# Attention's result turned by VectorE, queries and new keys loaded batch by batch, and layer 2 and 3's last products reordered

## The chip, the cores and the metric

The kernel runs on one core of one Trainium2 chip. The time is device microseconds of one execution; each kernel is run several times and the median is compared. TensorE (PE in the profile) multiplies, VectorE (DVE) and ScalarE (ACT) work on elements, GpSimd (POOL) works on elements and gathers rows, and SyncE (SP) mostly issues DMAs. Each engine runs its own list of instructions in order and waits on semaphores for the others.

## The reference

Four layers, each `x = x + ffn(cond(x))`, over 8 batches of 128 tokens of 512 features, all in float32. Layers 0 and 1 are gated and low-rank products. Layer 2 holds the attention, which takes most of the time, and layers 2 and 3 end with routed low-rank products. Cut to what the change touches:

```
# layer 2, conditioning: attention over a paged cache (32 query heads, 8 key heads of 128)
q, k, v = x @ Wq.T, x @ Wk.T, x @ Wv.T        # per head
q, k = rope(rmsnorm(q)), rope(rmsnorm(k))
k_all = concat(k_cache[block_table], k); v_all = concat(v_cache[block_table], v)
probs = softmax(mask(q @ k_all.T * SCALE))    # 512 cached and 128 new keys
y2 = (probs @ v_all) @ Wo.T
# layer 2, ffn, on y2
H = y2 @ W.T + b; z = y2 @ A
logits from H[:, 1::2, :8] and (z @ LiMEs.T)[:, 1::2]; weights = masked softmax, repeated over token pairs
x = x + H + (z * (weights @ LiMEs)) @ Bmat * 0.5
# layer 3, ffn: 64 experts of rank 8, 16 of them taken
out = (gated z) @ B_w.T * 2
x = x + out
```

## The kernel before

**Attention.** It runs in 32 steps: `steps` (qd, p) with eight key heads qd on the outside and four pairs of batches p on the inside, so step 4 qd + p. A step's TensorE work is, in this order: ten score products `st` of batch 0 of the pair (`weigh`, 128x512 each, four for cached keys and one for new keys, each in two records), the projection of the next step's queries, keys and values (`project`, tiles q_one, q_six, q_five), the last step's output product (`leave`, tiles wo_one, wo_two, wo_six), the scores of batch 1 mixed with the value products of batch 0, and the value products `av` of batch 1 (`mix`). Both products with weights use a seven-product scheme for 2x2 blocks (`seven`), whose sums of blocks are made by VectorE (`combine`). A float32 matmul shows as two records in the profile.

**Queries and new keys.** `rotate` puts a step's rotated queries (2 batches x 4 heads) and new keys (2 batches x 1) side by side in the tile r, all queries first. `turn` (L1206) transposes r with one VectorE stream transpose, which works on blocks of 32x32, and writes the result to the DRAM tensor turned_new in four DMAs; `fetch` (L1234) loads it back with the blocks in their places: one DMA of 512 KB for all queries (tile qT) and one of 64 KB for each batch's new key (tile kTn). qT and kTn have one buffer each, so a load of the next step's queries waits until the last scores of this step have read the old ones. Steps 0 and 1 are turned by TensorE instead (`turn_at_once`). The cached keys go the same way through turned_cached.

**The result.** y2 (8 batches of 128 tokens by 512, in SBUF) collects the output products. In the last four steps (qd = 7) each pair p - 1 is complete once step p has run `leave`; `run` then calls `end.turn` twice (L1497), which turns one batch with four TensorE transposes into PSUM and copies it to Y2T with VectorE or ScalarE. After the last step come the h products of quarter 0 (256 tokens) with W (`product`, 16 matmuls into the tiles h_0 and h_1), the last `leave`, the turning of the last pair (`layer2`), the products hdT for the anchors (`anchors`) and z (`low`), the routing on VectorE, and the h products of quarters 1 to 3.

**Order.** `kept` fixes an instruction's place in its engine's program order; instructions without it may be moved by the scheduler that builds the program. Before, the transposes y2T, hdT, z and h were not kept, and the scheduler put four of the h products of quarter 1 between the last transposes and the first hdT. DMAs that SyncE issues run in the order of its queue; after the last step it issues R (the softmax sums, `inverted`), then the loads of Bm, W, Wq, keys, wB3T, wmr, BwT (`open3`) and the sums for a check (L833).

**Layer 3's last products.** `Seven` (L2095) does four output blocks with seven products in two PSUM banks, odd and even. For tokens of group g = 1 two of them run one after the other, k = 0 and 1 (`last`, L2244): `go_on` multiplies, with VectorE forming u and p1 between the products, then x gets its sums, and the four blocks are added to x and each sent out by a DMA on SyncE's queue (L2258, L2259).

Of the kernel before, what the change touches and what calls it, by code (L numbers as in the profile page):

```python
# [17 lines left out]
P = 128  # L18
NB = 8
# [28 lines left out]
def forward(ctx: ExitStack, tc: tile.TileContext, a: dict, out: bass.AP):  # L48
# [31 lines left out]
    ))  # L80
    late_turned = w3T, wB3T, A2T
    down_turned, adapter_turned = (
# [794 lines left out]
def attention(tc, a, x, ident, lens, kvrow, part, ww, wop, ypool, sums, rot, eps, psa, c2, chunks, mm):  # L877
# [262 lines left out]
    def rotate(n):  # L1140

        both = wk.tile([P, 2 * REP + 2, HD], F32, tag="r", name=f"r_{n}", bufs=1)
        views = {"q": both[:, 0 : 2 * REP], "k": both[:, 2 * REP :]}

        def terms(m, t, nh):

            full = [P, 2, nh, HD]
            ws, wx = (w[:, pair(n), :] for w in tabs[m])
            r = views[m].rearrange("p (j h) d -> p j h d", j=2)
            u = wk.tile(full, F32, tag="v" + m, name=f"v{m}_{n}", bufs=1)  # L1150
            for b in ((slice(0, 1), slice(1, 2)) if nh > 1 else (slice(0, 2),)):
                for lo, hi in ((0, 64), (64, 0)):
                    to = u[:, b, :, lo : lo + 64]
                    kept(pool.tensor_tensor(  # L1154
                        to, t[:, b, :, hi : hi + 64],
                        wx[:, b, lo : lo + 64].unsqueeze(2).to_broadcast(list(to.shape)), ALU.mult,
                    ))
            def straight_terms():
                kept(dve.tensor_tensor(r, t, ws.unsqueeze(2).to_broadcast(full), ALU.mult))

            S[n]["r" + m] = r, u
            return straight_terms

        S[n]["both"] = both
        terms("q", S[n]["q"], REP)()
        return terms("k", S[n]["k"], 1)
# [39 lines left out]
    def turn(n, by=(sp,)):  # L1206

        s = S[n]
        m = 2 * REP
        t = wk.tile([P, 4, m + 2, 32], F32, tag="kt", name=f"qkt_{n}", bufs=1)  # L1210
        done = kept(dve.transpose(t, s["both"].rearrange("p m (b d) -> p b m d", b=4)))
        s["qT"] = wk.tile([P, 4, m, 32], F32, tag="qT", name=f"qT_{n}", bufs=1)
        s["kn"] = wk.tile([P, 2, 4, 32], F32, tag="kTn", name=f"kTn_{n}", bufs=1)
        written(turned_new[n], t, by)
        return done

    def turn_at_once(n):

        s = S[n]
        m = 2 * REP  # L1220
        s["qT"] = qT = wk.tile([P, 4, m, 32], F32, tag="qT", name=f"qT_{n}", bufs=1)
        s["kn"] = kn = wk.tile([P, 2, 4, 32], F32, tag="kTn", name=f"kTn_{n}", bufs=1)
        for h in (slice(0, REP), slice(REP, m), slice(m, m + 2)):
            k = h.stop - h.start
            ps = psa.tile([P, k, P], F32, name=f"turned_{n}_{h.start}", **(
                dict(tag="av") if n == 0 and k == REP else dict(tag="st", bufs=3)
            ))
            for i in range(k):
                kept(pe.transpose(ps[:, i, :], s["both"][:, h.start + i, :], ident))
            to = qT[:, :, h, :].rearrange("p a m t -> p m a t") if k == REP else kn  # L1230
            kept(act.copy(to, ps.rearrange("p m (a t) -> p m a t", t=32)))

    def fetch(n):
        s = S[n]  # L1234
        m = 2 * REP
        src = turned_new[n].rearrange("b i a m d -> (b i) a m d")
        kept(sp.dma_start(s["qT"], src[:, :, 0:m, :]))
        for j in range(2):
            kept(sp.dma_start(s["kn"][:, j], src[:, :, m + j, :]))

    def weigh(n, j, then={}):
# [5 lines left out]
        for c in range(NC):  # L1247
            ps = psa.tile([P, REP * P], F32, tag="st", name=f"st_{n}_{j}_{c}", bufs=3)
            kept(pe.matmul(  # L1249
                ps, s["kT"][:, c, 4 * j : 4 * j + 4, :] if c < 4 else s["kn"][:, j],  # L1250
                s["qT"][:, :, REP * j : REP * (j + 1), :].rearrange("p a i t -> p i a t"), start=True, stop=True,
            ))
# [149 lines left out]
    def run(pool_, end_of, bank, keep):  # L1402
# [11 lines left out]
        w_ops, wo_ops = iter(()), WO[0].factors()  # L1414

        def some(ops, k=1):
            return lambda: [next(ops, None) for _ in range(k)]

        for n, (qd, p) in enumerate(steps):
# [75 lines left out]
            if qd == NQ - 1 and p:  # L1495
                for j in range(2):
                    end.turn(y2, 2 * (p - 1) + j, bank)  # L1497
        divided(n)
        every(outputs(n))
        end.product(0, ("st", "st"), bank)  # L1500
        leave(n)
# [312 lines left out]
def ending(  # L1814
# [64 lines left out]
    def turn(y2, b, bank):  # L1879
# [3 lines left out]
        for c in range(DC):  # L1883
            pe.transpose(ps[:, c, :], y2[:, b, c * P : (c + 1) * P], ident)
        (act.copy if b % 2 else dve.tensor_copy)(Y2T[0][:, :, b * P : (b + 1) * P], ps)

    def quarter(q):
        return slice(q * NT // 4, (q + 1) * NT // 4)

    def low(bank):  # L1890

        ps = bank("mm", [P, NT // 4], "z2")
        for c in range(DC):
            for q in range(4):
                mmq(ps[slot(q), :], A2[:, c, :], Y2T[0][:, c, quarter(q)], c == 0, c == DC - 1)
        act.copy(zq, ps)

    def anchors(bank, meanwhile):

        ps = bank("mm", [P, P], "hdT")  # L1900
        for c in range(DC):
            for q in range(4):
                mmq(ps[slot(q), :], WH[:, c, :], Y2T[0][:, c, q * NT // 4 + 1 : (q + 1) * NT // 4 : 2], c == 0, c == DC - 1)
        hdT = L3.w3.tile([P, P], F32, tag="hdT", name="hdTs")
        dve.tensor_copy(hdT, ps)
        meanwhile()
        ps = bank("mm", [P, NA, 32], "hd")
        pe.transpose(ps.rearrange("p q e -> p (q e)"), hdT, ident)
        dve.tensor_tensor(hd, ps[:, :, 0:16], b16.unsqueeze(1).to_broadcast([P, NA, 16]), ALU.add)
# [7 lines left out]

    def product(q, tags, bank, at=range(2), begun=False):

        for i, tag in zip(at, tags):  # L1920
            ps = H[q, i] if begun else bank(tag, [P, 2, NT // 4], f"h_{q}_{i}")
            for o in range(2):
                for c in range(DC):
                    mmq(
                        ps[:, o, :], W["2"][:, c, (2 * i + o) * P : (2 * i + o + 1) * P], Y2T[0][:, c, quarter(q)],
                        not begun and o == 0 and c == 0, begun and c == DC - 1,
                    )
            H[q, i] = ps

# [165 lines left out]
    class Seven:  # L2095


        def __init__(self, name, bank, A, B):
            self.A, self.B = A, B
            self.even, self.odd = (bank("mm", [P, 2, 256], f"{name}_{i}") for i in range(2))  # L2100
            self.p1, self.u = (
                L3.w3.tile([P, 256], F32, tag=f"seven_{n}", name=f"{n}_{name}", bufs=2) for n in ("p", "u")
            )
            self.c = {(0, 0): (self.even[:, 0], None), (0, 1): (self.odd[:, 1], self.u),
                      (1, 0): (self.even[:, 1], self.u), (1, 1): (self.odd[:, 0], self.p1)}

# [4 lines left out]
        def begin(self):  # L2111
            self.into(self.even[:, 0], self.A[0], self.B[0], True)
            act.copy(self.p1, self.even[:, 0])

        def go_on(self):
            a11, a12, a22, s1, s2, s3, s4 = self.A
            b11, b21, b22, t1, t2, t3, t4 = self.B
            u, p1, even, odd = self.u, self.p1, self.even, self.odd
            self.into(odd[:, 1], s1, t1, True)
            self.into(odd[:, 0], s2, t2)  # L2120
            dve.tensor_tensor(u, odd[:, 0], p1, ALU.add)
            dve.tensor_tensor(p1, odd[:, 1], p1, ALU.add)
            self.into(even[:, 1], s3, t3)
            dve.tensor_tensor(p1, even[:, 1], p1, ALU.add)
            self.into(odd[:, 1], s4, b22)
            self.into(even[:, 0], a12, b21)
            self.into(even[:, 1], a22, t4)

# [110 lines left out]
    def last_begun(g, k, bank):  # L2239

        f = S["o", g, k] = Seven(f"o3_{g}_{k}", bank, S["b"][k], S["z", g])
        f.begin()

    def last(g, k):  # L2244
        f = S["o", g, k]
        f.go_on()
        for (i, j), (ps, more) in reversed(f.c.items()):
# [3 lines left out]
            if more is not None:  # L2251
                dve.tensor_tensor(t, t, more, ALU.add)
        for ij in ((1, 1), (0, 1), (0, 0), (1, 0)):
            ps = f.c[ij][0]
            o = 2 * k + ij[0]
            tok = slice(g * 512 + ij[1] * 256, g * 512 + (ij[1] + 1) * 256)
            t = x[:, o, tok]
            dve.tensor_tensor(t, ps, t, ALU.add)  # L2258
            sp.dma_start(out[o * P : (o + 1) * P, tok], t)  # L2259

    def layer2(y2, bank, do=range(NB)):

        for b in do:
            turn(y2, b, bank)
        anchors(bank, lambda: low(bank))
        where = ["mm"]
        folding = fold_scores(lambda tag, shape, name: bank(where[0], shape, name))
        if (0, 0) not in H:
            product(0, ("st", "st"), bank)
# [17 lines left out]
    def layer3(bank, between=lambda behind: None):  # L2287
# [31 lines left out]
        for k in range(2):  # L2319
            S["o", 1, k].B = S["z", 1]  # L2320
        last(1, 0)
        last(1, 1)

    return SimpleNamespace(
        prepare=prepare, load_w2=load_w2, load_aw=load_aw, turn=turn,
        product=product, shifted=shifted, open3=open3, layer2=layer2, layer3=layer3,
    )
# [65 lines left out]
```

## Time and profile before

| | us |
|---|---|
| median of three runs (1473.62 to 1477.49) | 1475.64 |
| the profiled execution | 1473.67 |
| its span, first to last instruction | 1471.8 |
| TensorE busy in it | 1459.9 |
| VectorE, GpSimd, ScalarE busy | 1066.8, 855.2, 559.0 |
| attention steps 2 to 30, start of the scores to the next | 364.43 to 1304.80 |
| 24 transposes y2T in the last three steps | 0.87, 0.88, 0.87 |
| SyncE waiting in `fetch` for turned_new's writes | 85.0 in 58 waits |
| end of the last value product (mix) | 1328.47 |
| end of the last output product of attention | 1342.29 |
| start of the last TensorE product | 1465.54 |

The page gives for each engine the busy time and its share of the span. The chain of waits goes back from the last instruction to what released it, step by step; a row is a start, a length and what ran. In the timeline a row is a start, a length, the engine and line, the operation, output and inputs with their shapes, and in brackets how long the engine stood idle before and for what. TensorE's records overlap, since matmuls are pipelined: a record of 0.59 us for 128x512 is followed by the next 0.43 us later. PEld is the loading of TensorE's stationary operand, which runs beside the products.

### The profile page before, as it was taken

To read this page: it belongs to the slowest core of one execution; us is meant where nothing else is said; L and a number is where in the kernel's file an instruction comes from. 1 tells how busy PE (TensorE), PEld (TensorE's weight loads), DVE (VectorE), ACT (ScalarE), POOL (GpSimd) and SP (SyncE) were. 2 spreads that over 40 slices of the span, in tenths; PEclk is the share of its full clock that TensorE was granted. 3 is DMA by queue.
4 is the path that set the end of the run, shared out by engine and by line. 5 is a ranking of instruction groups with operands and counts; after the bars stand their busy time and mean duration, and the time that the engine had idled before them with its cause. 6 is when DMAs were issued, how large, how long until landed. Compare 5 with 4: busy or idle time off the path is not lost.

```text
span 1471.8 us, 17654 instructions
## 1 busy us (share of the span) xinstructions
PE 1459.9 (99%) x5333; PEld 921.6 (63%) x5333; DVE 1066.8 (72%) x2128; ACT 559.0 (38%) x1416; POOL 855.2 (58%) x877
## 2 busy tenths in 40 slices
PE   9999999999999999999999999999999999999998
PEld 7888786455555555555565555556555555657886
DVE  4675535488878887877778787777878788875575
ACT  1111101044445544454554445455444444542110
POOL 2231104477767777777677777767777776731310
PEclk9999999999999999999999999999999999999999
DMA  7430312214655544464454456444445544343001
GB/s 244 131 76 26 73 35 70 90 39 123 178 157 165 156 121 129 150 184 129 136 151 120 126 157 184 129 137 150 117 129 155 173 137 134 115 122 99 1 9 52
DMA packets 178488, 177.02 MB, mean 120 GB/s; under 512 B 72336, under 2 KB 148208, under 8 KB 178256
## 3 DMA queue, kind: packets, MB, share of 16 engines
q1 hardware_dynamic: 160208, 138.79, 32.7%
q0 software_dynamic: 17056, 36.49, 8.0%
q8 instruction: 45, 0.74, 0.2%
q10 hardware_dynamic: 1120, 0.52, 0.1%
q14 instruction: 59, 0.48, 0.1%
HBM read 132.36 MB, written 43.11 MB: 119 GB/s over the span
## 4 chain that ended last, share of the span: by engine, by line
PE 91%; DMA 3%; DVE 3%; POOL 1%; issue 1%; ACT 0%; SPq 0%; ACTq 0%; DVEq 0%; POOLq 0%
PE st L1249 17%; PE av L1301 16%; PE g L414 9%; PE q_six L1055 8%; PE q_one L1055 5%; PE q_five L1055 5%; PE wo_two L1055 5%; PE dn L414 5%; PE wo_one L1055 4%; PE wo_six L1055 4%; PE eo_l L53 3%; PE h L1834 2%; PE z L1834 2%; PE o L1834 1%; PE midp_l L53 1%; DMA qT<-turned_new 1%
## 5 line engine op out<-in xcount | busy, mean ns | idle before, releaser
L998 POOL DMA_INDIRECT kn<-in_k_cache,kvrow_k x256 | 270.8, 1058 | 77.7 <-issue 67.1
L998 POOL DMA_INDIRECT vals<-in_v_cache,kvrow_v x256 | 273.1, 1067 | 73.6 <-issue 49.5
L1301 PE MATMUL av<-pT,vals 128*128 128x512 f32 x640 | 290.6, 593 | 0.2 <-DVE oT L1311 0.2
L1253 ACT ACTIVATE pT<-st,hide 128x512 f32<-128x512 f32 x256 | 175.9, 687 | 187.2 <-PE st L1249 187.1
L1249 PE MATMUL st<-qT,kT 128*128 128x512 f32 x512 | 236.2, 594 | 1.5 <-DMA qT<-turned_new 1.4
L1301 PEld LDWEIGHTS av<-pT,vals 128*128 128x128 f32 x640 | 121.6, 190 | 152.9 <-issue 146.9
L1154 POOL TENSOR_TENSOR vq<-q,txq 128x256 f32<-128x256 f32 x128 | 121.1, 977 | 131.5 <-ACT sqq L1128 89.9
L1249 PEld LDWEIGHTS st<-qT,kT 128*128 128x128 f32 x512 | 96.4, 190 | 111.2 <-issue 99.0
L1269 DVE TENSOR_TENSOR part<-pT 128x512 f32<-128x512 f32 x128 | 88.4, 691 | 77.6 <-ACT pT L1253 73.5
L1055 PE MATMUL q_one<-q,x 128*128 128x384 f32 x256 | 93.1, 486 | 0.0
L1128 ACT ACTIVATE sqq<-q 128x128 f32<-128x128 f32 x252 | 78.2, 310 | 11.8 <-DVE q L1104 5.1
L1055 PEld LDWEIGHTS q_one<-q,x 128*128 128x128 f32 x256 | 48.6, 190 | 39.7 <-issue 14.1
L1055 PE MATMUL q_six<-q_s,xs_all 128*128 128x384 f32 x192 | 69.8, 486 | 0.0
L1109 ACT COPY q<-q_one 128x256 f32<-128x256 f32 x32 | 11.9, 372 | 148.8 <-PE q_one L1055 142.7
L1055 PE MATMUL wo_one<-o,oT 128*128 128x256 f32 x256 | 65.7, 379 | 0.0
L1249 PE MATMUL st<-qT,kTn 128*128 128x512 f32 x128 | 65.4, 593 | 0.0
L1055 PE MATMUL wo_two<-o_s,os 128*128 128x256 f32 x256 | 60.6, 380 | 0.0
L1253 ACT ACTIVATE pT<-st,rs 128x512 f32<-128x512 f32 x64 | 44.0, 687 | 38.6 <-PE st L1249 38.6
L483 POOL TENSOR_TENSOR ws<-wu 128x256 f32<-128x256 f32 (+1 forms) x9 | 6.4, 711 | 87.7 <-DMA wu<-in_WuT 87.7
L1055 PEld LDWEIGHTS wo_one<-o,oT 128*128 128x128 f32 x256 | 48.7, 190 | 13.3 <-issue 0.5
L1285 ACT COPY rows<-rows 32x32 f32<-32x32 f32 x96 | 20.7, 216 | 93.1 <-DVE rows L1280 92.3
L414 PE MATMUL g<-xs,ws 128*128 128x256 f32 (+1 forms) x240 | 55.1, 379 | 0.0
(457 smaller groups left out, 2803.5 us busy)
## 6 DMA issues: line engine op xcount, KB each, us to landing
turned_new<-qkt SPq DMA_DIRECT2D x120, 160.0 KB
turned_cached<-kt SPq DMA_DIRECT2D x128, 128.0 KB
kT<-turned_cached SPq DMA_DIRECT2D x32, 512.0 KB
R<-sums SPq DMA_DIRECT2D x32, 512.0 KB
qT<-turned_new SPq DMA_DIRECT2D x30, 512.0 KB
q<-in_WqT SPq DMA_DIRECT2D x8, 1024.0 KB
o<-in_WoT SPq DMA_DIRECT2D x8, 1024.0 KB
kn<-in_k_cache,kvrow_k POOLq DMA_INDIRECT x256, 2.9
```

Of the source, the lines that this page charges most:

```text
L53: pe.matmul(o, lhsT, rhs, start=start, stop=stop)
L414: pe.matmul(o, lhsT, rhs, start=start, stop=stop, skip_group_check=True)
L998: kept(pool.indirect_dma_start(out=d[:, c, :], out_offset=None, in_=kc if what == "k" else vc, in_offset=bass.IndirectOffsetOnAxis(ap=kvro ...
L1055: kept(pe.matmul(o, l[:, c, :], r[:, c, :], start=start and c == 0, stop=c == 1, skip_group_check=True))
L1128: kept(act.activation(sq, S[n][m][:, j, i, :], AF.Square, accum_out=S[n]["ssq"][:, j, col : col + 1]))
L1154: kept(pool.tensor_tensor(to, t[:, b, :, hi : hi + 64], wx[:, b, lo : lo + 64].unsqueeze(2).to_broadcast(list(to.shape)), ALU.mult,))
L1249: kept(pe.matmul(ps, s["kT"][:, c, 4 * j : 4 * j + 4, :] if c < 4 else s["kn"][:, j], s["qT"][:, :, REP * j : REP * (j + 1), :].rearrange( ...
L1253: kept(act.activation(pT[:, c, :, :].rearrange("p i t -> p (i t)"), ps, AF.Exp, **(dict(bias=hide[:, b, c : c + 1]) if c < 4 else dict(bia ...
L1269: kept(dve.tensor_tensor(o, l, r, ALU.add))
L1285: kept(act.copy(rows[0:32, g, :], rows[32 * g : 32 * g + 32, 0, :]))
L1301: kept(pe.matmul(ps, v[:, c, :], pT[:, c, :, :].rearrange("p i t -> p (i t)"), start=c == 0, stop=c == NC - 1, skip_group_check=True,))
L1834: return pe.matmul(o, lhsT, rhs, start=start, stop=stop, skip_group_check=True)
```

## The change

Four things are changed.

1. y2 of the first three pairs is turned by VectorE (`turned_in`): one stream transpose per batch, four DMAs per batch that write it to a new DRAM tensor y2_turned in pieces of 128 bytes, and four per batch that load it into Y2T. The last pair is still turned by TensorE.
2. Transposes y2T, products hdT, z, hd and the h products of quarters 0 to 2 are kept in program order. Of the 16 h products of quarter 0, 12 run ahead of the last `leave`, three between it and the last pair's transposes, and one after them. In VectorE's order four sums of AwT stand together ahead of the copy of hdT, and the check of the sums stands ahead of zp.
3. r holds batch 0's queries and key and then batch 1's; qT and kTn are two tiles each, one per batch, and `fetch` loads queries and key of batch 0 first, then of batch 1.
4. For the last tokens the two `Seven` are interleaved: leading products of both, sums of both, then closing products and outputs of both. The second has a third PSUM bank for its product six, its last product and output are cut in halves of 128 columns, and three of the eight outputs are issued by ScalarE.

```diff
@@ attention @@
-        both = wk.tile([P, 2 * REP + 2, HD], F32, tag="r", name=f"r_{n}", bufs=1)
-        views = {"q": both[:, 0 : 2 * REP], "k": both[:, 2 * REP :]}
+        both = wk.tile([P, 2, REP + 1, HD], F32, tag="r", name=f"r_{n}", bufs=1)
+        views = {"q": both[:, :, 0:REP], "k": both[:, :, REP:]}
...
+    def new_turned(n):
+        S[n]["qT"], S[n]["kn"] = (
+            [wk.tile(shape, F32, tag=f"{what}{j}", name=f"{what}_{n}_{j}", bufs=1) for j in range(2)]
+            for what, shape in (("qT", [P, 4, REP, 32]), ("kTn", [P, 1, 4, 32]))
+        )
...
     def fetch(n):
-        s = S[n]
-        m = 2 * REP
         src = turned_new[n].rearrange("b i a m d -> (b i) a m d")
-        kept(sp.dma_start(s["qT"], src[:, :, 0:m, :]))
         for j in range(2):
-            kept(sp.dma_start(s["kn"][:, j], src[:, :, m + j, :]))
+            m = j * (REP + 1)
+            kept(sp.dma_start(S[n]["qT"][j], src[:, :, m : m + REP, :]))
+            kept(sp.dma_start(S[n]["kn"][j][:, 0], src[:, :, m + REP, :]))
...
+        def y2_turned(p):
+            bs = (2 * p, 2 * p + 1)
+            end.turned_in(y2, bs, lambda name: kvp.tile([P, 4, DC, 32], F32, tag="kn", name=name))
...
             if qd == NQ - 1 and p:
-                for j in range(2):
-                    end.turn(y2, 2 * (p - 1) + j, bank)
+                y2_turned(p - 1)
         divided(n)
         every(outputs(n))
-        end.product(0, ("st", "st"), bank)
+        end.product(0, ("st", "st"), bank, part=slice(0, 12))
         leave(n)
@@ ending @@
+    def turned_in(y2, bs, tile_of_turned):
...
+        for b in bs:
+            t = tile_of_turned(f"y2t_{b}")
+            kept(dve.transpose(t, y2[:, b, :].rearrange("p (c k i) -> p k c i", k=4, i=32)))
+            for q in range(4):
+                kept(sp.dma_start(
+                    late_turned[3][b, :, :, q], t[32 * q : 32 * q + 32].rearrange("i k c j -> i (k c) j")
+                ))
+        for b in bs:
+            for k in range(4):
+                kept(sp.dma_start(
+                    Y2T[0][slot(k), :, b * P : (b + 1) * P],
+                    late_turned[3][b, :, DC * k : DC * (k + 1)].rearrange("i c a j -> i c (a j)"),
+                ))
...
     def layer2(y2, bank, do=range(NB)):
+        begun = (0, 0) in H
+        if begun:
+            product(0, ("st", "st"), bank, part=slice(12, 15))
         for b in do:
             turn(y2, b, bank)
+        if begun:
+            product(0, ("st", "st"), bank, part=slice(15, 16))
         anchors(bank, lambda: low(bank))
...
     class Seven:
...
         def go_on(self):
+            self.lead()
+            self.close()
...
+            for h in (slice(0, P), slice(P, 2 * P)) if self.apart else (slice(0, 2 * P),):
+                self.into(six[:, h], a22, t4[:, :, h])
...
+    def last_out(g, k):
+        f = S["o", g, k]
         for ij in ((1, 1), (0, 1), (0, 0), (1, 0)):
...
+            n = P if f.apart and ij == (1, 0) else 2 * P
+            for h in range(0, 2 * P, n):
+                by = act if g and (ij == (0, 1) or h) else sp
...
-        last(1, 0)
-        last(1, 1)
+        both = [S["o", 1, k] for k in range(2)]
+        for k, f in enumerate(both):
+            f.lead()
+            summed_up(1, k)
+        for k, f in enumerate(both):
+            f.close()
+            last_out(1, k)
```

## The prediction

> **What bounds the kernel now.** First the page's head and the slices: TensorE is busy in 99% of the span at full granted clock, so only TensorE work removed, TensorE waits removed, or the tail after its last matmul can shorten the time.
>
> ```profile
> span 1471.8 us, 17654 instructions
> PE 1459.9 (99%) x5333; PEld 921.6 (63%) x5333; DVE 1066.8 (72%) x2128; ACT 559.0 (38%) x1416; POOL 855.2 (58%) x877
> PEclk9999999999999999999999999999999999999999
> ```
>
> Then the chain of work that ended last, in order of time (start, us, what), for the attention steps and their last groups:
>
> ```profile
> 651.95 4.35 DMA qT<-turned_new
> 656.34 4.56 PE st L1249 x10
> 688.85 4.29 PE st L1249 x10
> 721.09 4.29 PE st L1249 x10
> ...
> 1132.34 3.91 DMA turned_new<-qkt
> 1136.32 4.51 DMA qT<-turned_new
> 1140.88 4.56 PE st L1249 x10
> ...
> 1303.92 0.88 PE y2T L1884 x8
> ```
>
> An undisturbed step lasts 32.24 us (688.85 to 721.09). Where the scores (st, L1249) follow a DMA, the step before was longer: the load of the turned queries landed after TensorE had nothing else left. Last the timeline of TensorE's end and of the VectorE adds and SyncE output issues behind it:
>
> ```profile
> 1460.55 2.32 PE L1834 MATMUL o<-zs,Bws 128*128 128x256 f32 x10
> 1463.06 1.13 PE L1834 MATMUL o<-zgT,Bws 128*128 128x256 f32 x4 [0.18 <-DVE p_o L2122]
> 1464.02 1.03 PE L1834 MATMUL o<-zgT,BwT 128*128 128x256 f32 x4
> 1464.89 1.03 PE L1834 MATMUL o<-zs,BwT 128*128 128x256 f32 x4
> ```
>
> ```profile
> 1465.95 0.76 DVE L2258 TENSOR_TENSOR x<-o,x 128x256 f32<-128x256 f32 x2 [0.76 <-PE o L1834]
> ```
>
> ```profile
> 1465.32 1.54 SPq L2259 DMA_DIRECT2D out<-x  x1
> ```
>
> TensorE stands before 1463.06 for a VectorE add, the last two adds wait for its very end, and one output issue takes 1.54 us where its neighbours take 0.33 to 0.40.
>
> **Part 1, y2 turned by VectorE.** Three groups of eight transposes leave TensorE: 0.87 + 0.88 + 0.87 us at 1270.81, 1303.92 and 1328.47 in the chain, 2.62 us. In their place VectorE gets two stream transposes per group in place of one 0.69 us copy (nearest row, partT at L1279: 0.71 us for 128x512, so +0.7 us per group; ScalarE loses a 0.59 us copy), and SyncE's queue eight writes and eight loads. In the first two groups both are covered: the turned rows are needed a step or more later, and VectorE idles 0.45 to 2.2 us for ScalarE at the start of those steps. The cover that TensorE loses there is the 0.87 us behind which the next queries could land; part 2 must make good for it, else some 0.3 us per group comes back.
>
> The third group is the delicate one. Call M the end of the last mix (1328.47). Before, y2T 0.87 and 16 products h (32 records, 6.91) ran from M to the start of Wo's last group at M+7.8, and its 28 records ended at M+13.8. Now 12 of the 16 products come first: M+5.2. Wo's first product needs oT (its first half done at 1333.5, M+5.0), so it starts; its second needs the second left sum, which VectorE finished at 1335.03, M+6.6. TensorE thus stands about 0.6 us from M+6.0, and Wo ends at M+11.8. That is 2.0 us sooner, of which 1.73 us (four products of 0.43) is only moved behind Wo. So the third group brings 0.87 - 0.6 = 0.3 us, and the part 0.87 + 0.88 + 0.3 = **2.0 us**. Bounds: 0 (the waits eat it) and 2.6.
>
> [...]
>
> Is the third round trip hidden? The writes have the form of the late weights' (L644: 32 rows of 16 pieces of 128 B, issues 0.50 us long and 0.55 apart, and that stretch moved some 125 GB/s). SyncE is free at M+0.6, after R; eight issues end at M+5.0, just as fast as 512 KB flow at 125 GB/s (4.2 us); landing some 1.3 us later (A_turned, 234.6 to 235.9); eight loads at some 0.4 us each to M+8.2, landed near M+10.2. The anchors (hdT) need all quarters at Wo's end + 2.7 us (three h 1.30, eight transposes 0.87, one h 0.43), M+14.5. Slack 4.3 us. Behind it on SyncE's queue stand Bm, W, Wq, keys, wB3T, wmr, BwT and the sums, issued from 1329.08 to 1338.7 before, now 7.6 us later. The first reader is qwp at 1357.5, which moves to about 1355, and the loads took until 1343: still hidden. So is VectorE's new order of the AwT sums (four of 0.6 us ahead of the 0.29 us copy of hdT): that copy ends 5.6 us after Wo, the z products until 5.9.
>
> **Part 2, queries and new keys batch by batch.** All 30 loads of qT (512 KB) plus 60 of kTn become 60 of half that size and 60 of kTn: one issue of 0.52 us more per step on SyncE, which has over 1 us free before the next sums. The first half needs no release by the second batch's scores, and half the bytes. From 364.43 to 1304.80 are 29 steps, 940.4 us; less 29 x 32.24, alp (0.98) and y2T (1.75) leaves 2.7 us of waits; the first load adds 0.6 (av x16 from 356.93 should end at 363.80, st starts 364.43). Single waits are 0.05 to 0.7 us. The load takes 4.4 to 5.0 us; at the 380 GB/s that large loads reach, half of it saves 0.7 us plus the kTn ahead of its completion, about 1 us, more than any wait. The second half is due 17 us later. I take **2.9 us** (some restart cost may stay); bounds 0 and 3.3. The queries' buffer gets gaps (two runs of 512 in place of 1024); VectorE's nearest row with such runs, r<-r,rs with its broadcast (1.23 us), is no dearer than the plain r<-r,vq (1.21), so 0. The two extra ScalarE copies at steps 0 and 1: 0.27 x 2 - 0.37, under 0.2 us each, beside TensorE work.
>
> **Part 3, last groups interleaved.** Both groups' leading products run first, so the VectorE adds of one lie under the other. Wins: the stand before 1463.06 (10 records from 1460.55 end at 1462.71: 0.35) and its slow restart (0.96 for four instead of 0.86): 0.45. The split last product frees the third add early; two adds of 128 columns (0.28 each by vals 128x128) replace two of 256 (0.76): 0.25. Output issues on two queues: the last began 0.7 us after its add (1466.71 to 1467.42), now some 0.1: 0.6. Together **1.3 us**; bounds 0.4 (a 1.5 us issue again) and 1.6. ScalarE, which now issues three, is idle there.
>
> **Sum:** 2.0 + 2.9 + 1.3 = 6.2 us, 0.42%. The profiled execution took 1473.67 us (span 1471.8, 1.9 around it), 2.0 below the median of 1475.64; the same cut makes 1467.5 of it and 1469.4 of the median.
>
> **Rivals.** *The split brings nothing* (waits pass to the turned_new writes, 3.9 us ahead of the load): for it, two of the largest waits hang on qkt, the writes and the load in a row; against it, the load's own 4.5 us is the last link of each. Part 2 is 0, the cover of part 1 is missed (0.3): 6.2 - 2.9 - 0.3 = 3.0, 1472.6.
> *The fixed order and R eat part 1*: sum 4.2, 1471.4. For it: SyncE's and VectorE's rows above hide by 0.3 us only in one place; against: the other covers are 4 us wide.
> *Slower, by the third round trip*: the sixteen DMAs of the last step, on one queue and through one DRAM tensor, go one after another, each waiting for the landing before. At 0.5 + 1.3 us each they end 29 us after M+0.6, 15 us after the anchors are due: 6.2 - 15 = 9 us slower, 1484. It decides from a trip of 20 us on (M+14.5 + 6.2), against 9.6 worked out. Against it: the late weights' eight writes were issued 0.55 us apart without waits (209.56 to 213.7).
>
> **How the numbers follow.** About 0.3% (4.4 us) is what a measurement of this kernel tells from no change. Forecast 0.64, split without effect 0.14, part 1 eaten 0.10, slower 0.10 (half of it a small loss from causes I don't see), more than forecast 0.02. Forecast's own range 1466.0 to 1471.2; the two weak cases reach 1472.6 and the scatter of runs (1473.62 to 1477.49) adds 2, so 1466 to 1475. Faster 0.68, same 0.21, slower 0.11.
>
> **What would show it.** No wait of st on qT left, steps of 32.24 throughout; h directly behind the last mix and a stand of about 0.6 us inside Wo's last group; hdT not waiting for a DMA; no stand in the last 24 products, last output issue within 0.2 us of its add. The prediction is wrong if hdT waits for y2T's load, if st still waits for qT, or if the last output issue is held again.

## The result, and the profile after

The changed kernel took 1470.99 us (median of seven runs, 1468.32 to 1471.45), before beside it 1476.08 (seven runs, 1473.62 to 1479.72): a ratio of 0.996, 95% interval 0.995 to 0.997, 5.1 us less. The profiled execution took 1471.33 us, its span 1469.5 us, which is only 2.3 us below the profiled span of before. The median lies 1.6 us above the forecast of 1469.4 and 0.4 below the 1471.4 of the rival "part 1 eaten", so the time alone doesn't tell these two apart; the experiments have to.

The page of the changed kernel, its head and the slices of TensorE and its clock:

```profile
span 1469.5 us, 17710 instructions
...
PE 1456.8 (99%) x5313; PEld 919.3 (63%) x5313; DVE 1066.5 (73%) x2132; ACT 557.5 (38%) x1415; POOL 854.4 (58%) x877
...
PEclk9999999999999999999999999999999999999999
```

Still TensorE sets the time, busy 99% of the span at a granted clock of 0.998, and works 3.1 us less. The chain of waits that showed `st` behind `DMA qT` before can't be followed in this trace (below, why), so the list of TensorE's waits in the attention steps and layer 2 has to answer: engine, line and tile, what it waited for, us in total, how often, the longest. First before, then the changed kernel:

```profile
PE st L1249 <- DMA qT<-turned_new: 1.4, 3, 0.5
PE av L1301 <- DVE oT L1311: 0.2, 1, 0.2
```

```profile
PE q_five L1056 <- issue: 0.7, 1, 0.7
PE q_six L1056 <- issue: 0.6, 1, 0.6
PE wo_two L1056 <- DVE os L1015: 0.4, 1, 0.4
PE av L1307 <- DVE oT L1317: 0.2, 1, 0.2
```

The waits for queries are gone. The forecast stand in Wo's last group is there (wo_two). The two at the top were not forecast; they stand at 341 to 345 us. These lists leave out small waits and slow restarts (in before the four records behind the stand at 1463.06 took 1.13 us, the next four 1.03). Counted from the starts of TensorE's records, what exceeds the usual distance ahead of and inside `st` falls from 3.1 to 0.25 us.

The third group and the end, in the timeline of the changed kernel's TensorE (start, length, line, operation, tiles, shape, count, idle before and its releaser):

```profile
1325.45 5.34 PE L1843 MATMUL h<-y2T,WT 128*128 128x256 f32 x24
1330.63 1.03 PE L1056 MATMUL wo_one<-o,oT 128*128 128x256 f32 x4
1332.04 1.99 PE L1056 MATMUL wo_two<-o_s,os 128*128 128x256 f32 x8 [0.38 <-DVE os L1015]
...
1338.62 1.04 PE L1893 MATMUL y2T<-ident,y 128*128 128x128 f32 x8
1339.49 0.60 PE L1843 MATMUL h<-y2T,WT 128*128 128x256 f32 x2
1340.02 1.31 PE L1843 MATMUL hdT<-y2T,WH 128*32 128x128 f32 x31
```

```profile
1460.25 1.03 PE L1843 MATMUL o<-zgT,BwT 128*128 128x256 f32 x4
1461.11 1.05 PE L1843 MATMUL o<-zs,BwT 128*128 128x128 f32 x8
```

h follows the last mix at once, the stand begins 6.2 us later, and hdT at 1340.02 has no idle time ahead of it: the third round trip is hidden. The last products run without the stand that before had at 1463.06. The last add and the output issues behind them:

```profile
1462.20 0.49 DVE L2311 TENSOR_TENSOR x<-o,x 128x128 f32<-128x128 f32 x2 [0.47 <-PE o L1843]
```

```profile
L2312 SPq DMA_DIRECT2D out<-x x6: 332/404/1714, 1458.8 to 1463.3; - x6
L2312 ACTq DMA_DIRECT2D out<-x x3: 363/367/373, 1459.2 to 1462.8; - x3
```

Two halves of an add are done at 1462.69, 0.52 us after the last product (before 0.80), but one SyncE issue again takes 1.71 us (least, median and longest, in ns, stand ahead of the comma), and SyncE's last issue starts at 1463.26, 0.77 us after the half add that it belongs to (done at 1462.49). And the execution ends at 1469.5, 7.4 us after the last product, where before took 5.9.

### The profile page after: what moved, and what is told of

It reads as the page before. It is cut to its first block, busy times and chain, and to the rows that moved or that the text cites. A ratio compares the mean times of both kernels' runs of the same rounds, so it can differ in the third digit from the quotient of the medians.

```text
span 1469.5 us, 17710 instructions
## 1 busy us (share of the span) xinstructions
PE 1456.8 (99%) x5313; PEld 919.3 (63%) x5313; DVE 1066.5 (73%) x2132; ACT 557.5 (38%) x1415; POOL 854.4 (58%) x877
## 4 chain that ended last, share of the span: by engine, by line
```

## The experiments

The parts are those of the prediction: part 1 is changes 1 and 2, part 2 is change 3, part 3 is change 4. The medians of before lie up to 4.6 us apart on the three chips, so only kernels of one chip are compared: four on chip A (the expectations' "first chip"; before there: 1479.34, 1475.07 to 1484.05), four on B (1474.73, 1472.57 to 1477.81), four on C (1477.28, 1473.87 to 1481.97). What the profiles show is compared by stretches that hold the same work, in the table for all fourteen profiles, "before" and "changed" being the first two (us, from the starts of TensorE's records; "hold" is what the distances between starts exceed the usual ones from 340 to 350 us, a part of the first column; the last product's last record has 256 columns without part 3 and 128 with it):

| profile | first score to start of last av | last av to last h product | to the start of the last product | its end to the span's end | hold | span |
|---|---|---|---|---|---|---|
| before | 1014.87 | 44.88 | 92.78 | 5.9 | 0.3 | 1471.8 |
| before_again | 1015.48 | 44.88 | 92.78 | 7.4 | 0.1 | 1473.8 |
| interleave_only | 1013.52 | 44.88 | 92.45 | 6.4 | 0.1 | 1469.7 |
| split_only | 1014.67 | 44.88 | 92.78 | 6.0 | 2.9 | 1471.0 |
| turn_only | 1018.73 | 44.24 | 92.78 | 7.3 | 2.1 | 1476.0 |
| no_turn | 1011.79 | 44.88 | 92.45 | 6.6 | 0.2 | 1469.1 |
| no_turn_c | 1013.38 | 44.88 | 92.45 | 7.0 | 1.4 | 1471.5 |
| changed | 1012.30 | 44.44 | 92.44 | 7.4 | 2.1 | 1469.5 |
| after_again | 1012.33 | 44.33 | 92.45 | 6.8 | 2.2 | 1469.4 |
| changed_c | 1013.32 | 44.34 | 92.45 | 6.4 | 2.2 | 1470.6 |
| all_sync | 1012.49 | 44.26 | 92.44 | 6.4 | 2.2 | 1469.0 |
| all_sync_c | 1011.25 | 44.33 | 92.44 | 6.6 | 1.3 | 1467.8 |
| filled | 1010.67 | 43.76 | 92.44 | 5.9 | 0.1 | 1466.6 |
| filled_c | 1011.88 | 43.76 | 92.45 | 6.6 | 1.3 | 1468.9 |

### Chip A: after_again, all_sync, split_only, turn_only

**after_again** has no edit.

> The changed kernel itself, once more. Its first profile shows two losses that the forecast did not hold: TensorE stood twice between 341 and 345 us (0.86 and 0.79 us, with slow restarts 1.9 us in all), behind VectorE and ScalarE instructions that began only two groups of products after the group they wait for; and from the last product's end to the span's end it took 7.3 us where before took 5.9, one of the 16 DMA engines landing its part of the last outputs some 2.4 us after the others, with a code load of 16 KB (1.82 us) among them. Theory 'both are the program's': both come back, span 1469.5. Theory 'the first is chance, the second the program's' (the waits there are for the same counts in both programs; the second follows from ScalarE's late branch): span about 1467.6, the end again some 7 us. Theory 'both chance': span about 1466.2. Timed: some 5 us under before by the runs shown; 2.3 if the profiled pair is typical.

1470.19 us against 1479.34, ratio 0.9943 (0.9927 to 0.9958): 9.1 less where the first pair gave 5.1. Both unforecast losses came back in the profile: a hold in the waits (q_six, 1.7 us), and an end 6.8 us after the last product. The first theory seemed right; before_again, no_turn and filled below upset it.

**all_sync**, from the changed kernel:

```diff
-                by = act if g and (ij == (0, 1) or h) else sp
+                by = sp
```

> The changed kernel, but SyncE issues all the outputs and ScalarE none. Theory 'ScalarE's late exit': ScalarE, which has nothing left to do from about 8 us before the end, branches past the redo block early as it did before; its code load is then not among the last outputs, and VectorE's exit is not held by it. From the last product's end to the span's end 7.3 us become about 5.8 (last add 0.5, VectorE's exit 3.2, the closing chain 1.9), some 1.4 us less. Rival 'queue': three more issues of about 0.5 us behind the one of 1.7 us put the last issue 1.0 to 1.5 us later, and the end is as long as in the changed kernel or longer.

1471.54 us, ratio 0.9952 (0.9936 to 0.9968); its five runs, 1470.81 to 1471.72, lie 1.35 above after_again's in the median. In the profile ScalarE branches 10 us before the last product's end, early as said, and VectorE gets past its branch in 3.25 us (3.91 in the changed kernel). But the end came 6.4 us after the last product, not 5.8. So theory "late exit" is not borne out, and the profile (0.4 shorter) and the timed runs (1.35 longer) disagree. So it was run again on chip C.

**split_only** is before with the hunks of `rotate`, `turn`, `new_turned`, `turn_at_once`, `fetch` and `weigh`:

```diff
-        kept(sp.dma_start(s["qT"], src[:, :, 0:m, :]))
         for j in range(2):
-            kept(sp.dma_start(s["kn"][:, j], src[:, :, m + j, :]))
+            m = j * (REP + 1)
+            kept(sp.dma_start(S[n]["qT"][j], src[:, :, m : m + REP, :]))
+            kept(sp.dma_start(S[n]["kn"][j][:, 0], src[:, :, m + REP, :]))
```

> The kernel before, with part 2 alone: queries and new keys loaded batch by batch. Forecast: no wait of st on the load of qT is left, every step takes 32.24 us, and the time falls by 2.9 us (bounds 0 and 3.3): span 1468.9 against 1471.8. Rival 'the split brings nothing': the waits pass to the writes of the turned queries, 3.9 us ahead of the load, and the time is as before.

1473.30 us, ratio 0.9959 (0.9944 to 0.9973): 6.0 less. No wait for queries is in its list:

```profile
PE q_six L1055 <- DVE vals L1104: 2.4, 1, 2.4
PE av L1306 <- DVE oT L1316: 0.2, 1, 0.2
```

Less its hold, its attention stretch is 1014.67 - 2.9 = 1011.8; before's, less theirs, 1014.6 and 1015.4: 2.8 and 3.6 more. The rival (waits pass to the writes) is out. Timed it gains twice the forecast: the profile of before that the forecast was made from waited little.

**turn_only** is before with the hunks of `y2_turned`, `turned_in`, `turn`, `low`, `anchors`, `product` and `layer2`, no others.

```diff
-                for j in range(2):
-                    end.turn(y2, 2 * (p - 1) + j, bank)
+                y2_turned(p - 1)
...
-        end.product(0, ("st", "st"), bank)
+        end.product(0, ("st", "st"), bank, part=slice(0, 12))
```

> The kernel before, with part 1 alone: y2 turned by VectorE and the fixed order of layer 2, queries still loaded in one piece. Forecast: 2.62 us of transposes leave TensorE, a stand of 0.6 comes into the last group of Wo: 2.0 us less; but without part 2 the cover of the transposes is missed at two loads of queries, about 0.3 us each, so 1.4 to 2.0 less, and the waits of st on qT grow from 1.4 us in the list of waits to about 2. Rival 'order and round trip eat it': no gain, with hdT or z waiting for the load of y2T, or VectorE later than before at the steps where it turns y2.

1475.30 us, ratio 0.9981 (0.9969 to 0.9993): 4.0 less by the medians, 1.0 to 4.6 by the interval, which holds the forecast 1.4 to 2.0. Its profile waits more for queries than any other:

```profile
PE st L1250 <- DMA qT<-turned_new: 3.5, 5, 1.1
...
PE wo_two L1056 <- DVE os L1015: 0.2, 1, 0.2
PE av L1302 <- DVE oT L1312: 0.2, 1, 0.2
```

With restarts 6.8 us, against 3.1 and 3.9 in the two profiles of before; the line left out is its hold. All eight waits over 0.15 us stand between 365 and 1243 us, and VectorE first turns y2 at 1278, so it is not the lost cover of the transposes that shows here but how much the waits for queries differ from one execution to the next. Layer 2 is 0.64 shorter. What cover was lost can't be read from it.

### Chip B: before_again, interleave_only, filled, no_turn

**before_again** has no edit.

> The kernel before, unchanged, profiled once more. All five profiles taken since (the changed kernel twice, its all-SyncE form, split alone, turn alone) show TensorE held for 1.8 to 2.5 us at 341 to 345 us, at instructions that are the same in before, and before ran at 1475 to 1484 us beside them, above its profiled 1473.67. Theory 'the first profile of before was a fortunate execution': the hold of some 2 us is there too, and st waits longer for qT than the 1.4 us of the first list of waits (3.5 us in turn alone): span 1474 to 1480. Rival 'the change brought the hold': no hold at 341 to 345, span about 1472.

1474.78 us against 1474.73, ratio 0.9999 (0.9990 to 1.0009). No hold at 341 to 345, and 3.9 us of waits for queries with restarts, the largest at 363 us (1.1) where the first profile has it at 1140 (0.7). Its end took 7.4 us after the last product where the same program's first profile took 5.9: the end's length is no property of the program. The hold is missing, as the rival said; but it isn't of the change either, since filled and no_turn, below, have none.

**interleave_only** is before with the hunks of `Seven`, `last_begun`, `summed_up`, `last_out` and `layer3`.

```diff
-        last(1, 0)
-        last(1, 1)
+        both = [S["o", 1, k] for k in range(2)]
+        for k, f in enumerate(both):
+            f.lead()
+            summed_up(1, k)
+        for k, f in enumerate(both):
+            f.close()
+            last_out(1, k)
```

> The kernel before, with part 3 alone: last groups interleaved, outputs issued by SyncE and ScalarE. Forecast 1.3 us less: 0.45 on TensorE (no stand in the last 24 products), 0.25 from the halved last adds, 0.6 from the two queues. Theory after the profiles of the changed kernel: the 0.45 on TensorE stays, but the end from the last product to the span's end is no shorter, 6 to 7.3 us against 5.9, as ScalarE's exit and its code load fall among the last outputs: between 0.5 less and 1.0 more in the profile; timed, within the scatter of before (9 us), so the profile's last part decides.

1473.91 us, ratio 0.9998 (0.9988 to 1.0007): no difference that could be measured. TensorE's last stretch is 92.45 against 92.78, 0.33 less; the end after it, 6.4 us, lies between the two of before. Its queries still come in one piece, and of the four profiles without part 2 it waits least for them:

```profile
PE st L1249 <- DMA qT<-turned_new: 0.4, 1, 0.4
```

With restarts that is 2.0 us, and its attention stretch less its hold, 1013.4, is 1.6 us above split_only's.

**filled**, from the changed kernel:

```diff
         end.product(0, ("st", "st"), bank, part=slice(0, 12))
+        end.product(1, ("st", "av"), bank, part=slice(0, 2))
         leave(n)
...
-        product(1, ("st", "av"), bank)
+        product(1, ("st", "av"), bank, part=slice(2 if begun else 0, None))
```

> The changed kernel, with two products of the next quarter of h put between the twelve and Wo's last group. Theory: the stand at wo_two (0.5 to 0.65 us with its restart) is filled with work that is needed anyway, so the stand goes and nothing else moves: 0.5 us less, 1469.7 against the changed kernel's 1470.2. Rival: the sums that wo_two waits for hang on the same chain from the last mix, and the later start of wo_one passes the wait to the adds behind it and to the transposes of the last batches: no gain.

1468.42 us, ratio 0.9953 (0.9940 to 0.9967). In the timeline of its TensorE 28 records of h run ahead of Wo and nothing stands:

```profile
1324.72 6.21 PE L1844 MATMUL h<-y2T,WT 128*128 128x256 f32 x28
1330.77 1.03 PE L1056 MATMUL wo_one<-o,oT 128*128 128x256 f32 x4
1331.63 1.89 PE L1056 MATMUL wo_two<-o_s,os 128*128 128x256 f32 x8
```

Layer 2 takes 43.76 against 44.24 to 44.44 in the six other profiles with part 1: 0.5 to 0.7 less, as said; the wait is not passed on. Its program is the changed kernel's up to there, and it has no hold at 341.

**no_turn** is the changed kernel without part 1 (the hunks of split_only and interleave_only on before).

> The changed kernel without part 1: y2 turned by TensorE for all groups and the order left to the scheduler; parts 2 and 3 as changed. Forecast: part 1 is worth 2.0 us (2.62 of transposes less 0.6 of stand), so this runs 2.0 us above the changed kernel, 1472.2 against 1470.2. Rival 'order and round trip eat it': the same time as the changed kernel.

1470.66 us, ratio 0.9971 (0.9961 to 0.9982). Only one wait is left in its list:

```profile
PE av L1306 <- DVE oT L1316: 0.2, 1, 0.2
```

The changed kernel didn't run on chip B, so the 1472.2 and 1470.2 of the forecast can't be held against these times. On this chip interleave_only and no_turn differ by part 2 alone, 3.25 us, and no_turn and filled by part 1 with its stand filled, 2.24 us (2.0 and 0.5 forecast).

Against before no_turn is part 2 and part 3: 1011.79 for the attention steps, 3.1 and 3.7 under the two profiles of before. Filled takes 1010.67, and 0.5 of that is a wait of q_six for VectorE at 1280 us, in the step where VectorE first turns y2 (0.24 in the changed kernel, none in the other profiles with part 1). So the two covered groups of transposes are worth 1.1 us with that wait and 1.6 without, of the 1.75 expected. That part 1 brings this wait is not shown: q_six waits about as long at 1089 us in filled_c and at 639 us in changed_c, where y2 isn't turned.

### Chip C: the changed kernel beside three others

None of these four waits for queries, and yet each scatters by 2.2 to 7.0 us, not by little more than 1 us as expected below.

> The changed kernel beside the next three on one chip; none of the four waits for queries, so their times scatter by little more than 1 us and can be compared directly. Median near 1470, between no_turn_c and filled_c. If the hold at 341 to 345 us comes back only in profiles that lost part of their semaphore records (as in all five of five that had it, and in none of five complete ones), it is of that execution and not of the program.

> The changed kernel without part 1. By the parts of the profiles so far: transposes of two groups 1.7 us in the attention steps, 0.45 us net in layer 2: 2.2 above the changed kernel (forecast 2.0). Rival 'order and round trip eat it': the same time.

> The changed kernel with two products of the next quarter ahead of Wo's last group. By the profiles 0.6 us less than the changed kernel (last mix to last h product 43.76 us against 44.33 to 44.44). Rival 'the wait is passed on': same time.

> The changed kernel with all outputs issued by SyncE. On the first chip it took 1.35 us more than the changed kernel timed, while its profile ended 0.4 sooner; the end after the last product lasts 5.9 to 7.4 us in two profiles of one kernel, so a profile can't decide. Theory 'the second queue is worth its price' (forecast 0.6): 0.6 to 1.4 above the changed kernel. Theory 'ScalarE's late exit costs as much as the queue gains': the same time; 'costs more': below.

| | median, us | runs | to the changed kernel |
|---|---|---|---|
| changed_c | 1471.32 | 1470.36 to 1473.71 | |
| no_turn_c | 1473.07 | 1471.99 to 1476.34 | +1.75 |
| filled_c | 1470.94 | 1469.80 to 1472.02 | -0.38 |
| all_sync_c | 1471.23 | 1469.63 to 1476.62 | -0.09 |

Part 1 is worth 1.75 us by the medians, near the forecast 2.0, though the runs of the two overlap (1471.99 to 1473.71). The profiles agree: less the holds, no_turn_c's attention steps take 0.9 us more than changed_c's and 2.0 more than all_sync_c's, and its layer 2 0.54 more. So the rival of no effect is out. The ratios to before are 0.9957 (0.9941 to 0.9974) for the changed kernel and 0.9954 (0.9938 to 0.9970) for filled_c: the filled stand shows in both profiles (43.76), but timed it is inside the scatter, so that filled beats the changed kernel is shown by the trace and not by the clock. all_sync_c takes as long as the changed kernel: what chip A showed for the second queue (1.35) is not confirmed, and the worth of the second queue stays open (1.35 on chip A, -0.09 here).

## Why the prediction was right, and where it was not

The time fell inside the range of 1466 to 1475. The mechanisms of parts 1 and 2 held; of part 3 only TensorE's share did, and one more loss appeared that belongs to the execution. That 5.1 us came so near to 6.2 is in part luck: in the comparisons on chips A and C the same change gained 9.1 and 6.0.

**Part 2, forecast 2.9.** Mechanism and size held. In the traces of before and no_turn the load of the queries that a step's first scores need is issued 5.0 and 4.9 us ahead of them and lands 4.3 and 3.3 us after its issue (medians over the steps). So it is not issued earlier; it is 1.0 us shorter, about what was worked out for half the bytes at 380 GB/s (in four half microseconds of before in which such a load runs, from 685.95, 718.30, 751.72 and 782.82 us, the core's DMA moved 365 to 407 GB/s), and lands 1.6 us ahead of the scores in place of 0.5. In none of the ten profiles of kernels that load by batch does the list name a wait of st, and with restarts 0.2 to 0.6 us are left.

What the forecast did not see is that the waits of a kernel that loads in one piece are not a fixed 3 us: 2.0 in interleave_only, 3.1 and 3.9 in the two profiles of before, 6.8 in turn_only, in different steps. Beside split_only the part is thus worth 1.6 to 3.6 us by the stretches, and timed 3.25 between interleave_only and no_turn, 6.0 between before and split_only. The forecast scaled one execution's waits to the median; which execution had been profiled was luck.

The medians of before lie between 1474.73 and 1479.34 on the chips, those of the changed kernel between 1470.19 and 1471.32. Before scatters by 9.0, 5.2 and 8.1 us on chips A, B and C (18 to 24 runs), the kernels with part 2 by 0.9 to 4.4 (five to nine runs). But of the four kernels with eleven runs all_sync_c, which has part 2, scatters by 7.0 us and the three without it by 4.4 to 5.7, so that part 2 lessens the scatter is not shown.

**Part 1, forecast 2.0.** Two covered groups 1.1 to 1.6 us on chip B and 0.9 to 2.0 on C (expected 1.75), the third 0.44 to 0.64 net of the stand (forecast 0.3): 1.3 to 2.6 by stretches, 1.75 timed. The stand took 0.65 in the changed kernel, forecast 0.6. What the forecast left out of the third group is the fixed order: from Wo's last record to hd the same eighty records take 6.24 us before and 6.02 in the changed kernel, 0.2 less. Before, three of the four h products that the scheduler had moved stood among the last transposes and the fourth among the hdT products. The price that held for the transposes is 0.87 us for eight in the pipeline, though one record of them lasts 0.272 us (before, L1884).

The round trip took longer than worked out. In the changed kernel the eight writes took 5.44 us to issue and the eight loads 3.82:

```profile
1326.16 5.44 SPq L1904 DMA_DIRECT2D y_turned<-y2t  x8
1331.76 3.82 SPq L1909 DMA_DIRECT2D y2T<-y_turned  x8
1335.69 1.76 SPq L2059 DMA_DIRECT2D Bm<-in_Bmat  x4
```

that is 0.68 and 0.48 us each against 0.55 and 0.4 taken. In filled, whose records are complete, the last piece landed at 1336.66, 2.16 us after its issue began at 1334.50, and hdT started at 1339.50: a slack of 2.8 us where 4.3 was forecast. The term was mis-sized by 1.5 us under a cover that held. The rival "sixteen DMAs one after another" is out: the writes were issued 0.67 us apart.

**Part 3, forecast 1.3.** TensorE's 0.45 held: from the last h product to the end of the last product it takes 93.16 us in all four profiles without the part and 92.72 in all ten with it, 0.44 less (the starts in the table differ by 0.33 only, because the last record has half the columns).

The other 0.85, the halved adds (0.25) and the two queues (0.6), is the step that failed. What it was worked out from did come. The last add ended 0.5 us after the last product in place of 0.8, and the last output issue began 0.6 to 1.1 us after it in the eight profiles with ScalarE's help, 1.4 to 1.7 in the six with SyncE alone. But the end did not follow: from the last product's end to the span's end it takes 5.9 to 7.4 us (mean 6.6, six profiles) with SyncE's outputs alone and 5.9 to 7.4 (mean 6.6, eight profiles) with ScalarE's help. The forecast took the time from the last output's issue to its landing for fixed; in the fourteen profiles it is 2.3 to 4.2 us for SyncE's last output.

What ends the execution shows in SyncE's waits behind its branch past the redo block (us in total, times, longest), in before and then in the changed kernel:

```profile
SPq L850 <- SPq L850: 1.9, 4, 0.7
```

```profile
SPq L851 <- SPq L851: 3.7, 3, 3.0
```

There SyncE waits for the landing of the outputs. In before the last output landed at 1469.86; in the changed kernel the last but one of SyncE's landed at 1467.30, which is the wait of 3.0 us, and the last at 1467.45. About 2 us of closing steps follow. In all fourteen profiles SyncE is the last of VectorE, ScalarE and SyncE to reach the point at the very end where the engines wait for each other. In twelve the outputs' landing holds it. In filled and interleave_only, whose outputs had landed 3.4 us after the last product, it waits for ScalarE, which is past its branch only 4.9 and 5.4 us after that product. VectorE's way past its branch is long too, in before from 1466.59 to 1469.79, but VectorE is done there at 1469.90 and SyncE at 1470.96, so it does not end the execution.

Why the landing is late in some executions, stretches of 1 us of the changed kernel's end tell in part (us, busy of the engines, clock, share of the 16 DMA engines, GB/s):

```profile
1464.00:1465.00 1.00, 0.00 (x0) 0.00 (x0) 0.00 (x0) 0.00 (x0) 0.00 (x0) 0.84 0.55 167
1465.00:1466.00 1.00, 0.00 (x0) 0.00 (x0) 0.00 (x0) 0.00 (x0) 0.00 (x0) 0.50 0.08 13
1466.00:1467.00 1.00, 0.00 (x0) 0.00 (x0) 0.00 (x0) 0.00 (x0) 0.00 (x0) 0.50 0.06 14
```

From 1465 on the share is 0.06 to 0.08, little more than one engine of sixteen. 28 of the 32 parts of SyncE's last two outputs had landed by 1465.07, the other four between 1466.33 and 1467.45. A code load of 16 KB (the page's DMA queue q8, of the kind instruction) ran from 1463.99 to 1465.82, and the outputs' last packets from 1465.80 to 1466.88. The same stretches of before, whose outputs are nearly through at 1469 (15 of 16 parts of the last one landed by 1469.32):

```profile
1468.00:1469.00 1.00, 0.00 (x0) 0.00 (x0) 0.00 (x0) 0.00 (x0) 0.00 (x0) 1.00 0.72 230
1469.00:1470.00 1.00, 0.00 (x0) 0.00 (x0) 0.00 (x0) 0.00 (x0) 0.00 (x0) 1.00 0.04 14
```

The fourteen profiles part in the same way. Such a load runs near the end of each. In ten the outputs' last packet ended 0.4 to 1.1 us after the load, and the end took 6.4 to 7.4 us. In before, split_only, interleave_only and filled it ended ahead of the load's end, and the end took 5.9 to 6.4. That one or two DMA engines lag behind code loads fits all these numbers and is argued from them; no run took the loads away. The held issue goes with a load as well: in each of the fourteen one output issue of SyncE takes 1.1 to 1.8 us while another 16 KB load runs.

**The hold at 341 to 345 us** took 2.1 - 0.3 = 1.8 us of the gain between the first two profiles; without it their spans differ by 4.1 us in place of 2.3. It sits where VectorE and ScalarE wait for TensorE's count; in the changed kernel:

```profile
339.52 0.55 DVE L1069 TENSOR_TENSOR uq<-q_six,uq 128x384 f32<-128x384 f32 x1
341.97 0.56 DVE L1071 TENSOR_TENSOR uq<-q_five,uq 128x384 f32<-128x384 f32 x1 [1.90 <-PE q_one L1056]
```

uq needs q_five, done at 339.3, and starts 2.7 us later, with the end of q_one. The program is not the cause: no_turn and filled run without the hold on chip B and with 1.3 to 1.4 us of it on chip C.

**Which forecast values held.** By the stretches part 1 brings 1.3 to 2.6, part 2 1.6 to 3.6 and part 3 0.44, together 3.3 to 6.6, against 6.2 forecast and 5.1 timed. "Part 1 eaten" and "the split brings nothing" are out. Of the signs named to show it wrong, hdT waiting and st waiting did not come; "the last output issue is held again" did, in effect: an issue of 1.71 us stood three ahead of SyncE's last, which began 0.77 us after its add where 0.2 was forecast.

## What to carry to other kernels

The waits for the queries differed from one execution to the next, 2.0 to 6.8 us in the four profiles that load in one piece: take the worth of such waits from the spread of the timed runs as well as from one profile, and load what is due first by itself (0.2 to 0.6 us of waits were left). With TensorE busy 99% of the time, moving transposes that took 2.62 us in the pipeline to VectorE and DMA paid 1.75 us timed on chip C; the new order opened a stand of 0.65 us, and two independent products in it took layer 2 down by 0.5 to 0.7 us. Before pricing the last output's issue, follow the path to the very end: here it led through the landing, 2.3 to 4.2 us after the issue, and twice through ScalarE's way past a branch, 4.9 and 5.4 us after the last product.

## What the runs showed of the hardware that was not expected

**Lost semaphore records go with a hold.** In the profiles of before, before_again, interleave_only, filled and no_turn every count of TensorE is recorded (before: 1373 updates for 1370 instructions that make one). In the other nine about a quarter are missing (the changed kernel: 1060 for 1372), the chain of waits can't be followed, and all nine show TensorE held for 1.3 to 2.9 us at 340 to 350 us; the five complete ones lose 0.1 to 0.3 us there. What joins the loss and the hold no run here shows, and it is not settled that recording makes the hold. The same kernels also ran slower timed on chip C, where their profiles have it, than on B (no_turn 2.4 us, filled 2.5), but so did before (2.5).

**Code loads run among the last outputs.** From its branch at the very end to its next instruction VectorE took 2.9 to 4.3 us in the fourteen profiles, and the last of the 32 parts of SyncE's last two outputs landed 0.5 to 2.4 us after the 28th. Which engine a code load is for, and what takes VectorE so long there, the profile does not say.
